# One broadcast of 784 KB in place of eight of 98 KB, and two buffer rings resized, in a graph-network layer on one core

## The chip, the cores and the metric

The kernel runs on one core of one Trainium2 chip. The time is device microseconds of one execution; the lower is the better. An execution counts from the program's launch to its end, and the profile's span, from the first instruction to the last, is a little shorter.

## The reference, cut to what matters

```python
def _L0_gnn_ref(X, edge_index, edge_types, W_data, b_data, W_control, b_control, W_self, b_self):
    src, dst = (edge_index[0], edge_index[1])
    Xs = X[src]
    m_data = Xs @ W_data.T + b_data
    m_ctrl = Xs @ W_control.T + b_control
    msg = jnp.where((edge_types == 0)[:, None], m_data, m_ctrl)
    agg = jax.ops.segment_sum(msg, dst, num_segments=X.shape[0])
    out = agg + (X @ W_self.T + b_self)
    return jax.nn.relu(out)
...
x = _layernorm(x + _L0_gnn_ref(...), axis=-1)
```

X has 6250 nodes of 128 float32 values. There are 100000 edges, sorted by `dst`, with a random `src` and a random type of two. Each node sums the messages of its edges; a message is the source's row times one of two weight matrices.

## The kernel before, in words

**The message table.** For every node both possible messages are computed once, each split into three bfloat16 parts (`m3`, 128 x 98 x 384, kept in SBUF). A copy goes to DRAM as `table`, whose rows the gathers read.

**Two ways to sum.** Nodes 0 to 4319 are cut into 27 ranges of 160 nodes (`WN`), and these lie in eight groups of 1, 2 and six times 4 ranges (`GROUPS`). The other 1930 nodes are cut into 16 blocks of 125.

*A range* is summed with matrix products alone. `ranks` sorts a group's edges by their source tile: it builds one-hot matrices (`hots`, L691), counts with TensorE (L702), reads the slot of each edge from the counts on VectorE (L716), and scatters the edges' source and target numbers into a small matrix of 32 slots x 98 columns per range. That matrix, 6272 bytes for each range, is written to DRAM as `packed` (L772). `sums` then loads it back, broadcast to all 128 partitions, as the tile `rows` (128 x 3136 bfloat16, 784 KB; the ring has three buffers). VectorE turns `rows` into a one-hot matrix in place (L912, two halves). TensorE selects messages with it (L933, "stage 1"), the result is copied from PSUM (L436 on ScalarE or L437 on VectorE), and a second product with the one-hot matrix of the targets (`hot2`, L920; products L947 and L950) adds them up. Messages that did not fit a slot come in `gl`, copied from a gather (L861, L868).

*A block* is summed from gathered rows. GpSimd's indirect DMA fetches 128 rows of `table` at a time into a buffer `t_msg` (L1027, 263 gathers, 98 KB each). VectorE makes the one-hot matrices of up to six gathers at once in a buffer `t_hot` (L1021, 47 of them). TensorE multiplies the two (L1034).

**What sets the order.** Nothing is issued as it is written. Every step is handed to a planner (`Plan`, L92) with an engine, an estimated duration, a due time, the buffers that it reads and writes, and `lat`, an estimate of the time to its data. `Plan.run` (L136) lets each engine take, of the steps that it believes to be ready, the one that is due first; the order that results is fixed in the program. Each engine then works through its order strictly, and a step whose data are not there holds up all that stands behind it on that engine. For a load of `rows` the planner believes in 0.45 us of the SyncE queue (`SPD`, L274) for each transfer, and in 2.0 us (`lat`, L908) plus 0.12 us (`HOP`, L93) from there until another engine may use it. These constants are the same whatever the size of a transfer is.

```python
RP, RA, RS = 8, 14, 0.9
...
for j in range(RP):
    add("SP", SPD, lambda i=i, sp=sp, j=j: S.dma_start(
        sp.t[P // RP * j : P // RP * (j + 1)].rearrange("p r c -> p (r c)"),
        packed[gi, i // 2, (i % 2) * 64 : (i % 2) * 64 + R, :]
        .rearrange("r c -> (r c)")[None, :].to_broadcast([P // RP, R * NT])),
        due - RA + RS * j, [(packed_b, gi)], [(sp, ("p", j))], lat=2.0)
```

L912 of a range reads all of `rows`, so it waits for the last of its eight transfers.

Of the kernel before, what the change touches and what calls it, by code (L numbers as in the profile page):

```python
# [11 lines left out]
BF16 = mybir.dt.bfloat16  # L12
# [9 lines left out]
P = 128  # L22
D = 128
D3 = 3 * D
# [67 lines left out]
class Plan:  # L92
# [10 lines left out]
    def add(self, engine, dur, fn, due, r=(), w=(), lat=0.0):  # L103
        alts = engine if isinstance(engine, list) else [(engine, dur, fn)]
        op = Op(alts, due, lat)
        op.index = len(self.ops)
        kind = [(i[0] if isinstance(i, tuple) else i).name for i in w] or ["out"]
        if engine == "SP" and due > self.FROM:
            op.slack = self.SLACK.get(kind[0], 0.0)
        self.ops.append(op)  # L110
        deps = set()
        for items, writes in ((r, False), (w, True)):
            for item in items:
                b, key = item if isinstance(item, tuple) else (item, None)
                for k, (ws, rs) in b.keys.items():
                    if key is None or k is None or k == key:
                        deps.update(ws)
                        if writes:
                            deps.update(rs)
                if writes and key is None:  # L120
                    b.keys = {}
                ws, rs = b.keys.setdefault(key, ([], []))
                if writes:
                    b.keys[key] = ([op], [])
                else:
                    rs.append(op)
                if not b.users or b.users[-1] is not op:
                    b.users.append(op)
        deps.discard(op)
        op.deps = list(deps)  # L130
        return op
# [116 lines left out]
def sums_over_windows(ctx, tc, x, xt, edges, w, bias, out, total):  # L248
# [4 lines left out]
    work = ctx.enter_context(tc.tile_pool(name="work", bufs=2))  # L253
# [8 lines left out]
    def B(pool, shape, dtype, name, bufs=1, room=None):  # L262
        return Buf(plan, pool, shape, dtype, name, bufs, room)
# [8 lines left out]
    G0, G1 = 0.0, -4  # L272
    GC = 1.3
    SPD = 0.45  # L274
    RP, RA, RS = 8, 14, 0.9


    r0 = C([125, RH, 1], I32, "r0")
# [18 lines left out]
    def vec(due, cols, fn, r, w, rate=1.04):  # L297
        return add("DVE", dve(cols, rate), fn, due, r, w)
# [111 lines left out]
    def load_edges(b, n, out_, due, buf, key, engine):  # L410
        def fn():
            eng, typ = {"SP": (S, SP), "ACT": (A, ACT), "POOL": (G, mybir.EngineType.Pool)}[engine]
            if b:
                at = nc.values_load(
                    first.t[0:1, b : b + 1], engines=(typ,), min_val=0, max_val=E - n,
                    skip_runtime_bounds_check_because="it counts edges and is held to E - n")
                src = edges[ds(at, n), :]
            else:
                src = edges[:n, :]
            eng.dma_start(out_(), src.rearrange("(p k) c -> p k c", k=n // P))  # L420
        dur = (2.0 if engine == "POOL" else 1.6) if b else SPD
        add(engine, dur, fn, due, [first] if b else [], [(buf, key)], lat=2.0)
# [91 lines left out]
    def own(o, lhs, n):  # L514

        qs = [(j, min(R, n - R * j)) for j in range(-(-n // R))]
        for j, m in qs:
            T.matmul(o(j, m), lhs(j, m), w_sb.t[:, 2 * D :], start=False, stop=False,
                     skip_group_check=True)
        for j, m in qs:  # L520
            T.matmul(o(j, m), one3.t[:, :m], brows.t[:, 2 * D :], start=False, stop=False,
                     skip_group_check=True)
# [446 lines left out]
    def gathered(bis, when, step):  # L969

        nt, k_ = GT[bis[0]], len(bis)
        n = nt * k_
        gi = len(GROUPS) + bis[0]
        top = GB * max(GT)
        raw = B(work, [P, k_, nt, 3], I32, "t_raw", 2, 3 * top)
        for j, bi in enumerate(bis):
            load_edges(NW + bi, nt * P, lambda j=j: raw.t[:, j], when - 14 + 0.1 * j, raw, j,
                       "POOL" if bi < GB else "SP")
        G2 = lambda name, dt=F32: B(work, [P, k_, nt], dt, "t_" + name, 1, top)
        rel, lows, ins, far = (G2(k) for k in ("rel", "lows", "ins", "far"))  # L980
        cb, idx = G2("cb", I32), B(work, [P, n], I32, "t_idx", 2, top)
        code = B(work, [P, n, 2], BF16, "t_code", 2, 2 * top)
        d = when - 8
        nn = min(GN, N - NW * WN - GN * bis[0])
        fl = lambda b: b.t.rearrange("p b k -> p (b k)")
        f2 = lambda b: fl(b)[:, :, None].to_broadcast([P, n, 2])
        vec(d, n, lambda: V.tensor_sub(
            rel.t, raw.t[:, :, :, 1], gbase.t[:, bis[0] : bis[0] + k_, None].to_broadcast(
                [P, k_, nt])), [raw, gbase], [rel])
        vec(d, n, lambda: V.tensor_single_scalar(lows.t, rel.t, nn + 0.5, op=ALU.is_lt), [rel],  # L990
            [lows])
        vec(d, n, lambda: V.scalar_tensor_tensor(
            ins.t, rel.t, 0.5, lows.t, op0=ALU.is_ge, op1=ALU.mult,
            accum_out=counts.t[:, gi : gi + 1]), [rel, lows], [ins, (counts, gi)])
        vec(d, n, lambda: V.tensor_single_scalar(cb.t, raw.t[:, :, :, 0], 7,
                                                 op=ALU.arith_shift_right), [raw], [cb])
        vec(d, n, lambda: V.tensor_single_scalar(far.t, raw.t[:, :, :, 2], 0.0,
                                                 op=ALU.not_equal), [raw], [far])
        vec(d, n, lambda: V.tensor_add(far.t, far.t, cb.t), [far, cb], [far])
        vec(d, n, lambda: V.scalar_tensor_tensor(  # L1000
            idx.t.rearrange("p (b k) -> p b k", k=nt), far.t, 128.0, raw.t[:, :, :, 0],
            op0=ALU.mult, op1=ALU.add), [far, raw], [idx])
        vec(d, 2 * n, lambda: V.tensor_tensor(code.t, f2(rel), f2(ins), op=ALU.mult), [rel, ins],
            [code])
        KB = 6
        got = []
        for j, bi in enumerate(bis):
            n0 = NW * WN + bi * GN
            xc = B(work, [D, P], F32, "t_xc", 2)
            start = when + step * nt * j  # L1010
            add("SP", SPD, lambda xc=xc, n0=n0: S.dma_start(xc.t[:, :nn], xt[:, n0 : n0 + nn]),
                start, m3_key(NS - 1), [xc], lat=2.5)
            ga = B(ps, [P, 512], F32, "ga", 1)
            for k in range(nt):
                at = start + step * k
                kk = j * nt + k
                if k % KB == 0:
                    kn = min(KB, nt - k)
                    hot = B(work, [P, kn, P], BF16, "t_hot", 3, KB * P)
                    s4 = [P, kn, P // 2, 2]  # L1020
                    vec(at + 1, kn * P, lambda hot=hot, kk=kk, kn=kn, s4=s4: V.tensor_tensor(  # L1021
                        hot.t.rearrange("p k (c d) -> p k c d", d=2),
                        iota1_b.t[:, :P].rearrange("p (c d) -> p c d", d=2)[:, None]
                        .to_broadcast(s4), code.t[:, kk : kk + kn, None, :].to_broadcast(s4),
                        op=ALU.is_equal), [code, (iota1_b, 0)], [hot], 0.52)
                m = B(work, [P, D3], BF16, "t_msg", 11)
                add("POOL", GC, lambda m=m, kk=kk: G.indirect_dma_start(  # L1027
                    out=m.t, out_offset=None, in_=table[:, :],
                    in_offset=bass.IndirectOffsetOnAxis(ap=idx.t[:, kk : kk + 1], axis=0)),
                    at, [idx, table_b], [m], lat=3.0)  # L1030

                def mm(m=m, hot=hot, k=k, ga=ga):
                    for i in range(-(-nn // R)):
                        T.matmul(ga.t[R * i : R * i + R, :D3], hot.t[:, k % KB, R * i : R * i + R],  # L1034
                                 m.t, start=k == 0, stop=False, skip_group_check=True)
                add("PE", 0.165, mm, at + 4.5, [hot, m], [ga])
            end = start + step * nt + 6
            add("PE", 0.3, lambda ga=ga, xc=xc: own(
                lambda i, m: ga.t[R * i : R * i + m, :D],
                lambda i, m: xc.t[:, R * i : R * i + m], nn), end, [xc, w_sb, one3, brows], [ga])  # L1040
            got.append((ga, end))
        close("g", NW * WN + bis[0] * GN, nn, nn, got, [], end + 2)
# [184 lines left out]
```

## Time and profile before

| | |
|---|---|
| time, median of three runs (534.1 to 541.71) | 538.46 us |
| the profiled execution: its time / its span | 538.46 us / 536.9 us |
| TensorE products (PE), busy | 460.6 us, 86% of the span |
| VectorE (DVE), busy | 395.0 us, 74% |
| ScalarE (ACT), busy | 354.8 us, 66% |
| GpSimd (POOL), busy | 299.6 us, 56% |
| mean granted TensorE clock | 0.962 |
| loads of `rows` on the SyncE queue (L904) | 216 transfers of 98 KB |

The page gives, by engine, line and operation, the busy time, the mean duration, and the idle time before the instructions with what ended it. "A <- B" in the list of waits says that A stood idle until B had ended; three numbers follow: the sum in us, how often, and the longest. SPq is the SyncE queue, which issues nearly all plain transfers. A transfer's issue and its landing are separate: the queue goes on once the transfer is issued.

### The profile page before, as it was taken

To read this page: it belongs to the slowest core of one execution; us is meant where nothing else is said; L and a number is where in the kernel's file an instruction comes from. 1 tells how busy PE (TensorE), PEld (TensorE's weight loads), DVE (VectorE), ACT (ScalarE), POOL (GpSimd) and SP (SyncE) were. 2 spreads that over 40 slices of the span, in tenths; PEclk is the share of its full clock that TensorE was granted. 3 is DMA by queue.
4 is the path that set the end of the run, shared out by engine and by line. 5 is a ranking of instruction groups with operands and counts; after the bars stand their busy time and mean duration, and the time that the engine had idled before them with its cause. 6 is when DMAs were issued, how large, how long until landed. Compare 5 with 4: busy or idle time off the path is not lost.

```text
span 536.9 us, 27273 instructions
## 1 busy us (share of the span) xinstructions
PE 460.6 (86%) x11461; PEld 370.6 (69%) x11461; DVE 395.0 (74%) x1273; ACT 354.8 (66%) x889; POOL 299.6 (56%) x290
## 2 busy tenths in 40 slices
PE   5999966997789989898798999679979799769991
PEld 3665644865668878687587878468868677558980
DVE  6898976997879879797488996657948569363333
ACT  3565844674557868677376787456877558668991
POOL 1100077767575757567575667455776727776700
PEclk9999989998989999999799999798999989999997
DMA  4699797359782796629946288471597715975410
GB/s 132 188 245 349 236 154 188 99 137 172 145 160 58 146 195 141 178 54 158 189 113 166 56 166 174 107 172 45 122 174 150 169 31 119 184 151 143 96 45 19
DMA packets 66144, 76.87 MB, mean 143 GB/s; under 512 B 24024, under 2 KB 55917, under 8 KB 66013
## 3 DMA queue, kind: packets, MB, share of 16 engines
q1 hardware_dynamic: 52171, 47.36, 39.0%
q0 software_dynamic: 13456, 27.42, 23.3%
q8 instruction: 92, 1.51, 1.3%
q14 instruction: 39, 0.32, 0.2%
q10 hardware_dynamic: 386, 0.26, 0.2%
HBM read 60.50 MB, written 13.17 MB: 137 GB/s over the span
## 4 chain that ended last, share of the span: by engine, by line
PE 57%; DMA 20%; ACT 6%; DVE 6%; SPq 6%; issue 3%; POOL 1%; ACTq 0%; DVEq 0%
PE g L933 16%; PE a L947 15%; DMA rows<-packed 11%; PE rk L702 6%; PE ga L1034 6%; SPq L904 4%; ACT gs L436 3%; PE a L950 3%; PE vt L752 2%; ACT to_d L443 2%; DVE rows L912 2%; DMA gl<-sr 2%; DMA xr<-in_x 2%; PE g L493 2%; DMA t_msg<-table,t_idx 1%
## 5 line engine op out<-in xcount | busy, mean ns | idle before, releaser
L1027 POOL DMA_INDIRECT t_msg<-table,t_idx x263 | 280.3, 1066 | 186.1 <-PE ga L1034 76.1
L436 ACT CAST gs<-g 128x384 bf16<-128x384 f32 x640 | 275.0, 482 | 110.7 <-PE g L933 91.8
L947 PE MATMUL a<-gs,hot 128*32 128x384 bf16 x2592 | 258.6, 336 | 12.5 <-DVE gs L437 4.6
L933 PE MATMUL g<-m,rows 128*32 128x384 bf16 x2646 | 260.3, 336 | 3.1 <-DVE rows L912 1.3
L933 PEld LDWEIGHTS <-rows 128*32 128x32 bf16 x2646 | 166.4, 135 | 21.0 <-issue 6.8
L950 PE MATMUL a<-gs,hot 128*32 128x128 bf16 x1944 | 163.8, 222 | 1.7 <-issue 1.7
L947 PEld LDWEIGHTS <-hot 128*32 128x32 bf16 x2700 | 119.7, 97 | 37.7 <-issue 21.3
L1034 PE MATMUL ga<-t_msg,t_hot 128*32 128x384 bf16 x1036 | 104.8, 334 | 2.3 <-DMA t_msg<-table,t_idx 1.9
L950 PEld LDWEIGHTS <-hot 128*32 128x32 bf16 x2025 | 84.7, 98 | 8.2 <-issue 2.2
L702 PE MATMUL rk<-hots,rest 128*32 128x392 bf16 (+1 forms) x556 | 57.6, 331 | 33.5 <-DVE slot L716 32.6
L912 DVE TENSOR_SCALAR rows<-rows,pid 128x1568 bf16<-128x1568 bf16 x54 | 34.8, 657 | 68.1 <-DMA rows<-packed 38.0
L716 DVE TENSOR_REDUCE slot<-rk 128x4 f32<-128x392 f32 (+1 forms) x138 | 76.3, 553 | 11.1 <-PE rk L702 9.1
L920 DVE TENSOR_TENSOR hot<-iota_b,to_d 128x1280 bf16<-128x1280 bf16 (+1 forms) x81 | 67.4, 840 | 0.1
L702 PE MATMUL rk<-hots,tri 128*32 128x392 bf16 (+1 forms) x588 | 62.6, 328 | 1.4 <-issue 1.4
L702 PEld LDWEIGHTS <-rest 128*32 128x32 bf16 x624 | 25.7, 97 | 44.9 <-issue 42.5
L1034 PEld LDWEIGHTS <-t_hot 128*32 128x32 bf16 x1036 | 49.6, 99 | 8.5 <-issue 4.1
L691 DVE TENSOR_TENSOR hots<-iota_b,st 128x784 bf16<-128x784 bf16 (+1 forms) x83 | 39.1, 486 | 0.7 <-PE vt L752 0.6
L561 DVE TENSOR_REDUCE s<-a 128x128 f32<-128x384 f32 x27 | 15.0, 555 | 27.5 <-ACT bs L436 23.6
L1021 DVE TENSOR_TENSOR t_hot<-iota_b,t_code 128x768 bf16<-128x768 bf16 (+2 forms) x47 | 24.6, 523 | 10.6 <-PE ga L1034 8.9
L702 PEld LDWEIGHTS <-tri 128*32 128x32 bf16 x672 | 28.6, 99 | 4.3 <-issue 1.8
L752 PEld LDWEIGHTS <-two 128*64 128x64 bf16 x567 | 14.7, 111 | 7.4 <-DVE two L743 2.4
L861 POOL DMA_INDIRECT sr<-table,at x14 | 15.3, 1092 | 6.7 <-DVE at L849 3.0
(188 smaller groups left out, 528.0 us busy)
## 6 DMA issues: line engine op xcount, KB each, us to landing
rows<-packed SPq DMA_DIRECT2D x216, 98.0 KB
table<-m SPq DMA_DIRECT2D x12, 768.0 KB
t_msg<-table,t_idx POOLq DMA_INDIRECT x263
rows<-in_xt SPq DMA_DIRECT2D x8, 256.0 KB
xc<-in_xt SPq DMA_DIRECT2D x6, 320.0 KB
gl<-sr SPq DMA_DIRECT2D x27, 48.0 KB
xr<-in_x SPq DMA_DIRECT2D x5, 256.0 KB
out<-xr SPq DMA_DIRECT2D x5, 256.0 KB
```

What stands on the lines that cost most here:

```text
L436: [("ACT", act(cols), lambda: A.copy(o(), src())), ("DVE", dve(cols), lambda: V.tensor_copy(o(), src()))], None, None, due, r, w, lat)
L691: lambda k=k, kn=kn, ci=ci, hs4=hs4: V.tensor_tensor(hv(ci)[:, k - ks[ci] : k - ks[ci] + kn].rearrange("p k w (c d) -> p (k w) c d", d=2), ...
L702: T.matmul(acc.t[R * j : R * j + R, c * wide : c * wide + wide], wt.t[:, R * j : R * j + R], one(k).rearrange("p w c -> p (w c)"), start=s ...
L716: vec(due, len(m) * wide, lambda r=r, m=m: V.tensor_reduce(slot.t[:, r:KT:L, :], acc.t[:, : len(m) * wide].rearrange("p (k w c) -> p k w c ...
L752: T.matmul(vv()[q : q + 64, i // 2, :], two.t[:, (k - k0) * nw + i].rearrange("p f r -> p (f r)"), one(k)[:, i, :], start=k == 0 and i < 2 ...
L912: add("DVE", dve(half * NT, 0.335), lambda sp=sp, rs=rs: V.tensor_scalar(sp.t[:, rs], sp.t[:, rs], pid1.t, None, op0=ALU.is_equal), due - ...
L920: lambda i=i, hot2=hot2, s4=s4, c0=c0, c1=c1: V.tensor_tensor(hot2.t[:, c0:c1].rearrange("p g (c d) -> p g c d", d=2), iota1_b.t.rearrange ...
L933: T.matmul(gp.t[R * t : R * t + R, :D3], sp.t[:, :, 4 * g + t], m3.t[:, 4 * g + t, :], start=True, stop=True)
L947: T.matmul(a.t[R * j : R * j + R, :D3], hot2.t[:, g, R * j : R * j + R], gs.t, start=g == 0, stop=False, skip_group_check=True)
L950: T.matmul(a.t[R * c : R * c + R, D3:], hot2.t[:, g, P:], gs.t[:, c * D : (c + 1) * D], start=False, stop=last, skip_group_check=True)
L1027: add("POOL", GC, lambda m=m, kk=kk: G.indirect_dma_start(out=m.t, out_offset=None, in_=table[:, :], in_offset=bass.IndirectOffsetOnAxis(a ...
L1034: T.matmul(ga.t[R * i : R * i + R, :D3], hot.t[:, k % KB, R * i : R * i + R], m.t, start=k == 0, stop=False, skip_group_check=True)
```

## The change

Three constants differ. A range's `rows` is loaded by one transfer to 128 partitions instead of eight transfers to 16 partitions each (`RP` 8 to 1). The ring of `t_hot` has two buffers instead of three, and the ring of `t_msg` has fourteen instead of eleven. The planner runs again with these, so the order of all engines' instructions is made anew. With `RP` at 1 the due time of the one load is that of the first of the eight before (14 us ahead of the range's own due time).

```diff
-    RP, RA, RS = 8, 14, 0.9
+    RP, RA, RS = 1, 14, 0.9
...
-                    hot = B(work, [P, kn, P], BF16, "t_hot", 3, KB * P)
+                    hot = B(work, [P, kn, P], BF16, "t_hot", 2, KB * P)
...
-                m = B(work, [P, D3], BF16, "t_msg", 11)
+                m = B(work, [P, D3], BF16, "t_msg", 14)
```

## The prediction

> **What bounds the kernel now.** I read the page's busy times first, then the groups by line, the list of waits, the timeline of one load of `rows`, and the busy times of three stretches.
>
> ```profile
> PE 460.6 (86%) x11461; PEld 370.6 (69%) x11461; DVE 395.0 (74%) x1273; ACT 354.8 (66%) x889; POOL 299.6 (56%) x290
> ```
>
> TensorE is the busiest, and 536.9 - 460.6 = 76.3 us of the span are left in which it does nothing. No change of this kind makes its work shorter, so whatever is to be won lies in these 76.3 us. VectorE has 0.31 us of work an instruction (395.0 / 1273).
>
> ```profile
> L912 DVE TENSOR_SCALAR rows<-rows,pid 128x1568 bf16<-128x1568 bf16 x54 | 34.8, 657 | 68.1 <-DMA rows<-packed 38.0
> L716 DVE TENSOR_REDUCE slot<-rk 128x4 f32<-128x392 f32 (+1 forms) x138 | 76.3, 553 | 11.1 <-PE rk L702 9.1
> L1021 DVE TENSOR_TENSOR t_hot<-iota_b,t_code 128x768 bf16<-128x768 bf16 (+2 forms) x47 | 24.6, 523 | 10.6 <-PE ga L1034 8.9
> ```
>
> Behind the bar stand the busy time and the mean duration, behind the second bar the idle time ahead of the group: VectorE stood idle for 68.1 us ahead of the 54 halves of L912, twice the time that they work. The list of waits says what ended it, and who on TensorE then waited for VectorE:
>
> ```profile
> DVE rows L912 <- DMA rows<-packed: 38.0, 14, 4.8
> PE rk L702 <- DVE slot L716: 32.6, 16, 4.5
> DVE rows L912 <- DMA gl<-sr: 12.1, 4, 4.1
> DVE rows L912 <- DMA xc<-in_xt: 4.8, 1, 4.8
> PE a L947 <- DVE gs L437: 4.6, 2, 4.2
> DVE rows L912 <- DMA xr<-in_x: 4.3, 2, 4.1
> DVE rows L912 <- DMA t_xc<-in_xt: 4.0, 1, 4.0
> DVE rows L912 <- DMA t_raw<-in_edges: 3.1, 1, 3.1
> PE g L933 <- DVE rows L912: 1.3, 1, 1.3
> ```
>
> L912 reads nothing that arrives by `gl`, `xc`, `xr`, `t_xc` or `t_raw`; those transfers use the same semaphores, so I read all six rows as waits for `rows`: 38.0 + 12.1 + 4.8 + 4.3 + 4.0 + 3.1 = 66.3 us. The three rows of TensorE behind VectorE sum to 38.5 us, half of its 76.3. They are mostly not waits for `rows` itself: L702 needs the slot of L716, which stands behind L912 in VectorE's order. One case, from the timelines of SyncE, VectorE and TensorE:
>
> ```profile
> 65.09 10.42 SPq L904 DMA_DIRECT2D rows<-packed  x16
> 71.11 0.56 DVE L716 TENSOR_REDUCE slot<-rk 128x4 f32<-128x392 f32 x1
> 75.19 0.63 DVE L912 TENSOR_SCALAR rows<-rows,pid 128x1568 bf16<-128x1568 bf16 x1 [3.52 <-DMA rows<-packed]
> 76.21 0.56 DVE L716 TENSOR_REDUCE slot<-rk 128x4 f32<-128x392 f32 x1
> 76.82 0.52 PE L702 MATMUL rk<-hots,rest 128*32 128x392 bf16 x4 [3.65 <-DVE slot L716]
> ```
>
> SyncE begins a range's eight issues at 65.09. VectorE comes to L912 at 75.19 - 3.52 = 71.67, which is 6.6 us later, and stands still for 3.52 us. TensorE then stands still for 3.65. So 66.3 us of VectorE's stalls cost TensorE 38.5, a share of 0.58.
>
> **The part that matters: one transfer for eight.** It removes 189 of 216 issues. At 10.42 / 16 = 0.65 us each while they follow one another, the eighth is issued 4.6 us after the first; with one transfer that wait is gone. What does the data itself take? The stretches tell (columns: length, busy times of five engines, clock, share of the DMA engines' time, GB/s):
>
> ```profile
> 67.00:72.00 5.00, 4.82 (x135) 3.97 (x131) 4.67 (x10) 3.85 (x10) 2.98 (x2) 1.00 1.02 147
> 385.00:398.00 13.00, 11.31 (x327) 9.78 (x326) 8.01 (x23) 10.16 (x26) 10.26 (x10) 1.00 1.02 183
> 40.00:54.00 14.00, 13.28 (x150) 8.33 (x148) 12.60 (x30) 8.05 (x15) 0.00 (x0) 1.00 1.05 341
> ```
>
> The DMA engines' time is used up in all three (1.02 to 1.05), but they move 147 GB/s while the eight transfers of `rows` run and 341 when transfers to or from all 128 partitions run. In the packet records the 16 packets of a lone 16-partition transfer take about 0.3 us each, and 0.77 us when several follow. Two readings fit: the writes into so few partitions at a time are slow (then one transfer to 128 partitions runs at up to 341 GB/s), or the common source of 6272 bytes is (then it stays at 147).
>
> The fixed part comes from the chain:
>
> ```profile
> 216.89 3.93 DMA rows<-packed
> 287.81 3.21 DMA rows<-packed
> ```
>
> An eighth transfer with little ahead of it took 3.21 us from its issue to L912 (98 KB, 0.10 MB). One of 0.80 MB (784 KB) takes 3.21 + 0.70 / 341 = 5.3 us at best and 3.21 + 0.70 / 147 = 8.0 us at worst. I take 5.6, near the best, because a lone 16-partition transfer starts fast and slows down when more follow, which a slow source would not do. Before, from the first issue to L912 it was 10.1 us here (75.19 - 65.09).
>
> But the planner does not know this. By its constants the data are there 8 x 0.45 + 2.12 = 5.7 us after the first issue, and now 0.45 + 2.12 = 2.6 us after the only one. It puts L912 there if VectorE has nothing due sooner. In the built order the first range of groups two to eight has its L912 now 5, 14, 21, 9, 10, 7 and 8 VectorE instructions earlier, 10.6 on average, or 3.3 us. For these seven ranges VectorE came 6.6 to 8.7 us after the first issue, 7.7 on average; now 4.4. Against 5.6 us a stall of 1.2 us stays, 7 x 1.2 = 8.4. The second range of a group is now issued right behind the first, 0.45 us later, instead of after seven more issues; it lands about 0.70 / 341 = 2.1 us after the first, and its L912 stands some ten instructions (3.1 us) behind the first's, so nothing stays. Third and fourth ranges wait for a free buffer of `rows` as before, and their L912 is not moved ahead; 0. The very first range keeps its 1.3. Sum: 9.7 us of 66.3 stay, 56.6 go, and TensorE gains 56.6 x 0.58 = 32.8 us.
>
> What becomes of them? TensorE held up less comes sooner to its other waits. No row prices that; the bounds are nothing and all of it, and I take three tenths back, nearer to nothing since VectorE and ScalarE have a quarter and a third of their time free. That leaves 23 us.
>
> The removed issues on SyncE also let the transfers queued behind them (`gl`, `xb`, `win`, `out`) go some 4 us sooner. TensorE's one wait for `gl` is 3.1 us; I count nothing. One cost on the other side: 0.80 MB now stand as one block ahead of the table and x loads at 29 us and of gathers elsewhere. Gathers have room: in the trace they are issued 5 to 24 us ahead of their first product, and TensorE waited for one for 1.9 us in all. I count nothing; without that cover it would be 2 to 5 us at up to 27 places.
>
> [...]
>
> [...]
>
> **The two rings.** With fourteen `t_msg` buffers GpSimd runs further ahead. It waits 76.1 us for L1034 now, but is busy only 56% and TensorE waits 1.9 us for it: 0. With two `t_hot` buffers, 45 of the 47 fills must come after the products of the group but one before, not but two. In the trace each fill stands right behind the products that free its buffer, and 9 us or more ahead of its own; one group is 442 / 47 = 9.4 us, so the data still come in time. VectorE's wait there is 10.6 us now (the row of L1021); I take it unchanged.
>
> **Sum.** 538.46 (the profiled execution, which is also the median; 1.6 outside its span) - 23 = 515 us.
>
> **Rivals.** *The source is the limit.* The transfer takes 8.0 us. The seven stalls are 8.0 - 4.4 = 3.6 each, 25 us; second ranges land 4.8 us after the first and stall about 2 each, 14 us; with 1.3 about 41 stay, 25 go, x 0.58 x 0.7 = 10: 528 us. For it: 147 GB/s holds in a stretch with almost no other traffic. Against: the fast first packets.
>
> *The waits are only passed on.* TensorE is then held by ScalarE, its own order or the clock: 538 us. For it: ScalarE's copies (L436) take 482 ns where the code's plan has 375. Against: ScalarE is idle a third of the time.
>
> *The smaller `t_hot` ring costs more than is won.* VectorE's six waits at L1021 average 10.6 / 6 = 1.8 us. If all 45 later fills wait so, VectorE loses 81 us, TensorE 47, and 515 + 47 = 562 us. From 22 waits on (23 / 0.58 / 1.8) the kernel is slower than before. For it: each fill now follows products that are one group younger. Against: the planner places the fills anew, and only four rows of before were real stalls.
>
> **How the numbers follow.** The forecast has 0.60, the slow source 0.18, waits passed on 0.12, the smaller ring 0.10. The range goes from all 66.3 us won with nothing back (538 - 38 = 500) to 537, which takes in the slow source and part of the third case. Two per cent is 11 us (about what a measurement tells): below 527.7 lie nine tenths of the forecast and half of the slow source, 0.64; slower than 549 is the ring's case, 0.10; the rest, 0.26, is the same.
>
> **What would show it.** Right: idle time ahead of L912 near 10 us, all of it at the first range of a group; "PE rk <- DVE slot" below 12; some 300 GB/s while `rows` lands. Wrong: that rate near 147; L912 still above 40; or L1021's idle time above 40.

## The result and the profile after

The changed kernel takes 481.02 us (median of four executions, 478.18 to 483.65); the kernel before takes 540.09 us beside it (534.1 to 542.47). The ratio is 0.8938, with a 95% interval of 0.883 to 0.9047: faster. The forecast was 515 us with a range of 500 to 537; it had the side right and the size far too small. (Ratios set aside the executions of a kernel that lie over 1.5% above its fastest, here some of the kernel before, so they stand a little nearer to one than the medians' quotient.)

The profiled execution took 478.18 us, with a span of 476.5. From the page of the changed kernel, the busy times and the granted clock in 40 slices:

```profile
PE 442.0 (93%) x11461; PEld 362.7 (76%) x11461; DVE 393.0 (82%) x1271; ACT 354.1 (74%) x891; POOL 298.4 (63%) x290
PEclk9999999999999999999999999999999999999996
```

For the same clock line of the kernel before, look at the eights and sevens in it:

```profile
PEclk9999989998989999999799999798999989999997
```

The span is 536.9 - 476.5 = 60.4 us shorter, in two parts. TensorE stands still for 476.5 - 442.0 = 34.5 us where it was 76.3: 41.8 us. And it works for 442.0 us where it was 460.6, with the same 11461 products: 18.6 us. The forecast had reasons for the first part and had excluded the second ("no change of this kind makes its work shorter").

The groups by line and the list of waits of the changed kernel answer to the rows shown of before:

```profile
L912 DVE TENSOR_SCALAR rows<-rows,pid 128x1568 bf16<-128x1568 bf16 x54 | 34.2, 638 | 8.9 <-DMA rows<-packed 8.8
L1021 DVE TENSOR_TENSOR t_hot<-iota_b,t_code 128x768 bf16<-128x768 bf16 (+2 forms) x47 | 24.6, 523 | 11.8 <-PE ga L1034 11.6
```

```profile
DVE rows L912 <- DMA rows<-packed: 8.8, 6, 2.7
...
PE rk L702 <- DVE slot L716: 3.2, 6, 1.6
...
PE g L933 <- DVE rows L912: 1.3, 1, 1.3
...
PE a L947 <- DVE gs L437: 0.6, 1, 0.6
```

VectorE's idle time ahead of L912 is 8.9 us (before 68.1). TensorE's three waits for VectorE are 3.2 + 1.3 + 0.6 = 5.1 us (before 38.5). The row of L1021 is where it was (10.6 before).

Where did the 18.6 us of TensorE's work go? The clock records of the kernel before hold eight stretches at a granted clock of 0.50 ahead of its end, at 76.0, 127.2, 157.9, 260.3, 338.8, 362.7, 431.0 and 482.2 us. Six are 3.4 us long and two 6.8, together 34.1 us. The profiled execution of the changed kernel has none of these, only the one at its end that both have. The one at 338.8, in the busy times of two stretches of the kernel before (columns: length, busy times of five engines with their instructions, clock, share of the DMA engines' time, GB/s), and what stands right ahead of it on TensorE's timeline:

```profile
338.80:345.60 6.80, 4.83 (x78) 3.21 (x81) 6.19 (x16) 2.87 (x7) 2.59 (x3) 0.50 0.37 112
346.00:352.80 6.80, 6.73 (x182) 5.62 (x175) 4.50 (x10) 5.69 (x15) 3.14 (x4) 1.00 0.42 109
```

```profile
335.50 0.36 PE L933 MATMUL g<-m,rows 128*32 128x384 bf16 x4
...
335.88 0.36 PE L933 MATMUL g<-m,rows 128*32 128x384 bf16 x3
340.77 0.52 PE L702 MATMUL rk<-hots,rest 128*32 128x392 bf16 x4 [4.52 <-DVE slot L716]
341.05 0.56 PE L933 MATMUL g<-m,rows 128*32 128x384 bf16 x4
```

TensorE stood still for 4.52 us because VectorE was late; the clock fell during that wait; four products of L933 then took 0.56 us, where four had taken 0.36 before it. Over the whole execution the products of L933 and L947 last 526 ns where they lie wholly inside those stretches and 329 elsewhere, 1.6 times and not twice as long. TensorE is busy for 29.8 of the 34.1 us; an estimate of what the half clock cost is 29.8 x (1 - 329 / 526) = 11 us.

That leaves some 7 of the 18.6 us. Most of it lies in how busy time is counted: at full clock a product adds 0.31 us to it in the mean behind a gap and 0.04 us in a stream, and the kernel before has 63 gaps where the changed one has 46, which is 17 x 0.27 = 4.6 us. The rest is not assigned. So a stall of TensorE was paid more than once here: while it stood, and, where the clock fell, again while it worked on slowly.

When does the clock fall? In the clock records of before all eight stretches begin on one grid of 3.41 us. In the piece of that grid just ahead of each, TensorE was idle for 2.1 to 3.1 us, and in no other piece at full clock, from 11 us on to the last products, was it idle for more than 1.92. (In the four kernels of the square below the border lies in the same place, between 1.85 and 1.95 us, with one exception, a stretch behind a piece with 1.44.) So the length of one stall doesn't settle it: a stall of 1.32 us at 125.3 us, with smaller gaps beside it, was followed by a stretch, and one of 3.07 us at 84.7 us, which lies half in one piece and half in the next, was not. These are the pieces (idle is the length less the first busy time):

```profile
123.80:127.21 3.41, 1.31 (x24) 0.68 (x24) 2.69 (x11) 0.20 (x1) 2.80 (x3) 1.00 1.05 170
82.84:86.25 3.41, 1.49 (x37) 1.05 (x37) 2.59 (x8) 0.78 (x2) 2.51 (x3) 1.00 0.83 195
86.25:89.67 3.42, 1.87 (x49) 1.57 (x52) 1.14 (x3) 1.14 (x4) 2.51 (x4) 1.00 0.59 158
```

### The profile page after: what moved, and what is told of

Same layout as the page of the kernel before. It is cut to its first block, busy times and chain, and to the rows that moved or that the text cites. A ratio compares the mean times of both kernels' runs of the same rounds, so it can differ in the third digit from the quotient of the medians.

```text
span 476.5 us, 26926 instructions
## 1 busy us (share of the span) xinstructions
PE 442.0 (93%) x11461; PEld 362.7 (76%) x11461; DVE 393.0 (82%) x1271; ACT 354.1 (74%) x891; POOL 298.4 (63%) x290
## 4 chain that ended last, share of the span: by engine, by line
PE 73%; DVE 10%; ACT 7%; DMA 6%; issue 2%; SPq 0%; ACTq 0%; DVEq 0%
PE g L933 20%; PE a L947 19%; PE rk L702 9%; PE ga L1034 7%; ACT gs L436 4%; PE a L950 3%; PE vt L752 3%; DMA t_msg<-table,t_idx 3%; PE g L493 3%; DMA rows<-packed 2%; DVE hot L920 2%; PE a L493 2%; ACT to_d L443 2%; DVE slot L716 2%; PE ga L702 1%
## 5 line engine op out<-in xcount | busy, mean ns | idle before, releaser
L947 PE MATMUL a<-gs,hot 128*32 128x384 bf16 x2592 | 249.0, 328 | 7.7 <-ACT gs L436 5.1
L933 PE MATMUL g<-m,rows 128*32 128x384 bf16 x2646 | 253.0, 327 | 1.8 <-DVE rows L912 1.3
L933 PEld LDWEIGHTS <-rows 128*32 128x32 bf16 x2646 | 168.7, 134 | 13.1 <-DVE rows L912 1.6
L950 PE MATMUL a<-gs,hot 128*32 128x128 bf16 x1944 | 159.6, 219 | 0.2 <-issue 0.2
L947 PEld LDWEIGHTS <-hot 128*32 128x32 bf16 x2700 | 115.9, 95 | 33.9 <-issue 15.5
L1034 PE MATMUL ga<-t_msg,t_hot 128*32 128x384 bf16 x1036 | 102.0, 326 | 1.3 <-DMA t_msg<-table,t_idx 1.3
L716 DVE TENSOR_REDUCE slot<-rk 128x4 f32<-128x392 f32 (+1 forms) x138 | 76.3, 553 | 12.5 <-PE rk L702 9.8
L950 PEld LDWEIGHTS <-hot 128*32 128x32 bf16 x2025 | 82.5, 97 | 3.5 <-issue 0.4
L702 PE MATMUL rk<-hots,tri 128*32 128x392 bf16 (+1 forms) x588 | 59.9, 317 | 0.0
L702 PE MATMUL rk<-hots,rest 128*32 128x392 bf16 (+1 forms) x556 | 54.4, 320 | 4.9 <-DVE slot L716 3.2
L1034 PEld LDWEIGHTS <-t_hot 128*32 128x32 bf16 x1036 | 49.9, 97 | 5.5 <-issue 2.2
L912 DVE TENSOR_SCALAR rows<-rows,pid 128x1568 bf16<-128x1568 bf16 x54 | 34.2, 638 | 8.9 <-DMA rows<-packed 8.8
L1021 DVE TENSOR_TENSOR t_hot<-iota_b,t_code 128x768 bf16<-128x768 bf16 (+2 forms) x47 | 24.6, 523 | 11.8 <-PE ga L1034 11.6
L752 PE MATMUL vt<-hots,two 128*64 128x98 bf16 x546 | 17.1, 208 | 0.8 <-DVE two L743 0.4
```

The source lines that it names most:

```text
L702: T.matmul(acc.t[R * j : R * j + R, c * wide : c * wide + wide], wt.t[:, R * j : R * j + R], one(k).rearrange("p w c -> p (w c)"), start=s ...
L716: vec(due, len(m) * wide, lambda r=r, m=m: V.tensor_reduce(slot.t[:, r:KT:L, :], acc.t[:, : len(m) * wide].rearrange("p (k w c) -> p k w c ...
L752: T.matmul(vv()[q : q + 64, i // 2, :], two.t[:, (k - k0) * nw + i].rearrange("p f r -> p (f r)"), one(k)[:, i, :], start=k == 0 and i < 2 ...
L912: add("DVE", dve(half * NT, 0.335), lambda sp=sp, rs=rs: V.tensor_scalar(sp.t[:, rs], sp.t[:, rs], pid1.t, None, op0=ALU.is_equal), due - ...
L933: T.matmul(gp.t[R * t : R * t + R, :D3], sp.t[:, :, 4 * g + t], m3.t[:, 4 * g + t, :], start=True, stop=True)
L947: T.matmul(a.t[R * j : R * j + R, :D3], hot2.t[:, g, R * j : R * j + R], gs.t, start=g == 0, stop=False, skip_group_check=True)
```

## Experiments

The theory after the result: the one transfer does all of it, by taking away VectorE's stalls at L912 and with them the half-clock stretches. Rivals: the new order does it; the two rings do it; and, inside the first theory, it may be that there are fewer issues or that the writes go to all partitions at once.

The times differ from chip to chip. On one, the kernel before took 538.92 us, as in its first profile; on four others it took 678 to 689. So each kernel is compared with the kernel before on its own chip only. Each of these five chips was used at one time only, so the chip and the time are not told apart.

**A square: transfer and order, each alone.** First the changed kernel again.

> The changed kernel once more, beside the kernel before on this chip, as the mark for the three others here. If TensorE runs without the short gaps of its own that the last four runs showed (some 90 us of them), 481 us against 538 within 8 each. If it has them here too, the kernel before is near 690 us and this one at 0.98 to 1.0 of it, since the stalls at L912 then hide behind TensorE.

Then the one transfer in the order of before, with before's rings. The planner still believes in eight transfers; seven issue nothing:

```diff
-  add("SP", SPD, lambda i=i, sp=sp, j=j: S.dma_start(
-      sp.t[P // RP * j : P // RP * (j + 1)].rearrange("p r c -> p (r c)"),
+  add("SP", SPD, lambda i=i, sp=sp, j=j: j == 0 and S.dma_start(
+      sp.t.rearrange("p r c -> p (r c)"),
...
-      .rearrange("r c -> (r c)")[None, :].to_broadcast([P // RP, R * NT])),
+      .rearrange("r c -> (r c)")[None, :].to_broadcast([P, R * NT])),
```

> The order of before to the instruction, the first of a range's eight loads carrying all 784 KB. Theory A (the transfer makes the gain, in whatever order): within 10 us of the changed kernel on this chip, idle time ahead of L912 below 10 us. Theory C (the new order and the rings make it): nearer to the kernel before than to the changed one, above 510 us where that is 481 and 538.

And the reverse: order and rings of the changed kernel, but its one step issues the eight old transfers:

```diff
-  add("SP", SPD, lambda i=i, sp=sp, j=j: S.dma_start(
+  add("SP", SPD, lambda i=i, sp=sp: [S.dma_start(
-      sp.t[P // RP * j : P // RP * (j + 1)].rearrange("p r c -> p (r c)"),
+      sp.t[16 * k : 16 * (k + 1)].rearrange("p r c -> p (r c)"),
...
-      .rearrange("r c -> (r c)")[None, :].to_broadcast([P // RP, R * NT])),
+      [None, :].to_broadcast([16, R * NT])) for k in range(8)],
```

> The order of the changed kernel to the instruction, each load as eight transfers to 16 partitions. Theory A: not faster than the kernel before, 535 to 560 us where that takes 538; idle time ahead of L912 65 us or more, TensorE busy 458 us or more for the same products, clock at most 0.965. Theory C: 510 us or less.

**Eight transfers, but each to all partitions.** Order, rings and bytes of before. Each of the eight now writes an eighth of the columns (784 bytes) of all 128 partitions, where it wrote all 6272 bytes of 16 partitions:

```diff
-  sp.t[P // RP * j : P // RP * (j + 1)].rearrange("p r c -> p (r c)"),
...
-  .rearrange("r c -> (r c)")[None, :].to_broadcast([P // RP, R * NT])),
+  sp.t.rearrange("p r c -> p (r c)")[:, 392 * j : 392 * (j + 1)],
...
+  [None, 392 * j : 392 * (j + 1)].to_broadcast([P, 392])),
```

> The order of before to the instruction and eight transfers of 98 KB a range as there, but each goes to all 128 partitions (784 bytes of each) instead of all 6272 bytes of 16 partitions. Theory D (slow writes into few partitions at a time make the 147 GB/s): the rate while rows lands rises above 220 GB/s, idle time ahead of L912 falls to 10 to 25 us and the time to 485 to 505. Theory S (eight issues, whatever they carry): the idle time stays above 50 us and the time above 525.

What was measured, all on the same chip (before: median 538.92, 530.15 to 542.03, 13 executions; its profile is the first one):

| kernel | median us | ratio [95%] | idle ahead of L912, us | PE busy, us | PE idle, us | mean clock |
|---|---|---|---|---|---|---|
| before | 538.92 | | 68.1 | 460.6 | 76.3 | 0.962 |
| changed, again | 480.83 | 0.9011 [0.8924, 0.9098] | 7.2 | 443.6 | 37.3 | 0.988 |
| one transfer, order of before | 485.98 | 0.914 [0.9005, 0.9275] | 0.0 | 444.8 | 36.8 | 0.984 |
| eight transfers, order of after | 533.57 | 0.9967 [0.9896, 1.0038] | 70.9 | 461.0 | 73.8 | 0.962 |
| eight over all partitions, order of before | 504.42 | 0.9486 [0.9338, 0.9634] | 31.7 | 452.3 | 50.4 | 0.98 |

The one transfer is worth 538.92 - 485.98 = 52.9 us in the old order and 533.57 - 480.83 = 52.7 in the new. Order and rings together are worth some 5 us in either pair, and by the intervals that can't be told from nothing: with eight transfers the interval holds 1, with one transfer the two intervals overlap. The rivals "order" and "rings" fall as the cause of the large gain (the two were changed together here, so they are not told apart on this chip). What theory A expected held in both, but for 533.57 us where 535 or more were expected. The group of L912 in the profiles of one transfer in the old order, and of eight in the new:

```profile
L912 DVE TENSOR_SCALAR rows<-rows,pid 128x1568 bf16<-128x1568 bf16 x54 | 34.5, 652 | 0.0
```

```profile
L912 DVE TENSOR_SCALAR rows<-rows,pid 128x1568 bf16<-128x1568 bf16 x54 | 35.0, 654 | 70.9 <-DMA rows<-packed 47.5 <-DMA win<-in_edges 7.1 <-DMA out<-xr 6.4
```

In the old order no stall is left at all, which fits an L912 that has not been moved ahead; in the new order, 7 to 9 us are, as forecast, and the kernel is none the slower for it. The stretches at half clock (without the one at the end) follow: one in the changed kernel again, one with one transfer in the old order, eight (30.7 us) with eight transfers in the new order, three in the fourth kernel. So the second payment goes with the stalls, not with the order. With one transfer, the one stretch left in each of the two stands behind a wait of TensorE for a gather, of 2.7 and 3.1 us.

The fourth kernel was to part the two ways in which one transfer could help. Its order and its number of transfers are those of before, and 538.92 - 504.42 = 34.5 us of the 52.9 are won, about two thirds (60% by the ratios): so much goes with the spread of the writes over all partitions. The other 18 us go when eight issues become one. The parting is not clean, since the pieces written also shrink from 6272 to 784 bytes. And neither theory held whole: the time lies where theory D had it, but 31.7 us of idle time are more than its 10 to 25, and the rate, shown below, is not above 220 GB/s but 164. What the eight issues still cost is seen on its SyncE timeline, two ranges' issues in a row:

```profile
65.24 9.27 SPq L904 DMA_DIRECT2D rows<-packed  x16
```

How fast the data move, in the busy times of the stretch in which the second group's first two ranges land: first the changed kernel, then one transfer in the old order, eight over all partitions, and eight old transfers in the new order.

```profile
68.00:72.80 4.80, 3.09 (x83) 2.40 (x79) 2.64 (x7) 2.24 (x6) 3.22 (x4) 1.00 1.01 339
```

```profile
67.20:72.50 5.30, 5.12 (x139) 4.12 (x131) 5.30 (x12) 3.88 (x10) 3.66 (x4) 1.00 0.95 324
```

```profile
67.00:73.00 6.00, 5.74 (x160) 4.50 (x151) 5.93 (x13) 4.25 (x11) 4.10 (x3) 1.00 0.53 164
```

```profile
68.00:75.00 7.00, 1.98 (x52) 1.43 (x44) 0.37 (x2) 2.16 (x5) 4.93 (x6) 0.93 1.01 157
```

The last two columns are the reading. 157 GB/s at a share of 1.01: the DMA engines are full and slow. 164 GB/s at 0.53: they are half empty, the queue hands out transfers too slowly for them (9.27 / 16 = 0.58 us for each 98 KB allows no more than 173 GB/s). The rate is much the same in both, but in the fourth kernel the data land closer behind their issues: of these two ranges, the last packet was done at 77.7 us, and at 80.9 us in the kernel before, with the issues begun at 65.2 and 65.1. 324 to 339 at 0.95 to 1.01: full and fast. In the packet records, a packet of 6272 bytes takes 520 ns in the median before and 240 ns after.

**On the other chips.** Here each part was tried alone. One transfer alone is the kernel before with only `RP` at 1 (order made anew); rings alone has only `t_hot` at 2 and `t_msg` at 14; "planner told" is the changed kernel with the estimate of a load raised:

```diff
-  due - RA + RS * j, [(packed_b, gi)], [(sp, ("p", j))], lat=2.0)
+  due - RA + RS * j, [(packed_b, gi)], [(sp, ("p", j))], lat=4.6)
```

First chip, with the two kernels of the square:

> Kernel before with the one transfer of 784 KB alone; the rings stay at 3 (t_hot) and 11 (t_msg). Theory A (the transfer is all of it): idle time ahead of L912 near 9 us, granted clock near 0.99, 481 us within 8. Theory B (the rings, or the order that they bring, give a good part): 492 us or more, with GpSimd waiting for L1034 near 76 us as before.

> Kernel before with the two rings alone (t_hot 2, t_msg 14), eight transfers as before. Theory A: idle time ahead of L912 stays at 60 to 70 us, 538 us within 8. Theory B: 528 us or less. If the smaller t_hot ring costs something, the idle time ahead of L1021 rises above 20 us and the time above 546.

> The order is that of the changed kernel, to the instruction; each of its 27 loads is issued as eight transfers to 16 partitions, one behind the other. Theory A: L912 stands 3.3 us sooner in VectorE's order at the first range of a group, so the idle time ahead of L912 is at least that of before, 65 to 90 us; 540 to 560 us, granted clock 0.96 or less, TensorE busy 458 us or more for the same products (it is 442 in the changed kernel). Theory C: 505 us or less.

> The order of all engines is that of before, to the instruction; of a range's eight loads the first now carries all 784 KB to 128 partitions and the other seven are not issued. Theory A (the transfer itself): VectorE comes to L912 7.7 us after the issue on average and the data need 5 to 6, so the idle time ahead of L912 falls below 10 us; 481 us within 8, clock near 0.99. Theory C (the new order makes the gain): 505 us or more.

Second chip:

> The changed kernel, as the mark for the three others here: 481 us within 4, idle time ahead of L912 7 to 9 us.

> The changed kernel with one constant more: the planner is told that the load of rows takes 4.6 us (lat) instead of 2.0, close to the 4.0 to 5.5 us from issue to the last packet of a load with nothing ahead of it. Theory P (the 7 to 9 us left ahead of L912 at first ranges of groups still cost): idle time ahead of L912 below 3 us, and 3 to 8 us less than the changed kernel, 473 to 478. Theory Q (TensorE is the bound now, so the rest is covered, or the new order takes it back): within 3 us of the changed kernel, or slower.

> The kernel before with the one transfer alone, planned as such; rings 3 and 11. If the two rings make the 5 us between the changed kernel (481) and the one transfer in the order of before (486), this one is near 486; if the order that the planner makes for one transfer does, it is near 481.

> The kernel before with the two rings alone, eight transfers. If the rings are worth 5 us, 534 against 539; if not, 539 within 4. A cost of the smaller t_hot ring would show as idle time ahead of L1021 above 20 us and a time above 545.

Third chip:

> The changed kernel as the mark: 481 us within 4 where the kernel before takes 539; near 1.02 of the kernel before where that takes some 680.

> The changed kernel with the planner told 4.6 us instead of 2.0 for the load of rows. Theory P (the left stall costs): idle time ahead of L912 below 3 us, 3 to 8 us less than the changed kernel. Theory Q (covered, or given back by the new order): within 3 us of it, or slower.

> One transfer alone, rings 3 and 11. Rings make the 5 us: near 486. The order for one transfer makes it: near 481.

> The two rings alone, eight transfers. Rings make the 5 us: near 534. Not the rings: 539 within 4.

Fourth chip:

> The changed kernel with the planner told 4.6 us instead of 2.0 for the load of rows, against the changed kernel's 0.901 of the kernel before. Theory P (the left stall costs): 0.885 to 0.895 of the kernel before, idle time ahead of L912 below 3 us. Theory Q (covered or given back): 0.897 or more. Where the kernel before takes some 680 us, 1.01 to 1.02 of it.

> The two rings alone, eight transfers. Rings make the 5 us: 0.99 of the kernel before. Not the rings: 1.00 within 0.006. Where the kernel before takes some 680 us, 1.02 of it as in the two calls so far.

| ratio to before [95%] | first (before 689.48) | second (678.03) | third (688.19) | fourth (686.22) |
|---|---|---|---|---|
| one transfer alone | 0.9904 [0.9873, 0.9936] | 0.9953 [0.9925, 0.9982] | 0.9887 [0.9848, 0.9926] | |
| one transfer, order of before | 0.9901 [0.9869, 0.9933] | | | |
| rings alone | 1.0161 [1.0119, 1.0204] | 1.0219 [1.0161, 1.0278] | 1.0176 [1.0152, 1.02] | 1.016 [1.0098, 1.0222] |
| eight transfers, order of after | 1.0139 [1.0088, 1.0189] | | | |
| changed kernel | | 1.0179 [1.0127, 1.023] | 1.0111 [1.0069, 1.0154] | |
| changed kernel, planner told | | 1.0238 [1.0181, 1.0295] | 1.0191 [1.0122, 1.026] | 1.017 [1.0118, 1.0222] |

None of these chips gave the times of the first result, so they don't answer its question, but they show that the gain hangs on more than the transfer. Where an expectation named such chips for a part (1.02 for the rings, 1.01 to 1.02 with the planner told), it held. The changed kernel is 1.1 to 1.8% slower than before there. One transfer is worth only 0.5 to 1.1%, and the rings cost 1.6 to 2.2%. Where the kernel spends its time there, in the same 60 us of the changed kernel, first on the chip of the square, then on the third of these:

```profile
200.00:260.00 60.00, 58.56 (x1646) 49.84 (x1639) 53.37 (x162) 47.38 (x120) 45.86 (x45) 1.00 0.55 162
```

```profile
200.00:260.00 60.00, 46.06 (x1044) 32.28 (x1037) 36.50 (x126) 32.59 (x83) 26.53 (x27) 0.91 0.33 101
```

TensorE gets through 1044 products instead of 1646. That VectorE, fed by it, therefore comes to L912 later fits what follows, but was not tried by itself. This is the group of L912 with eight old transfers (rings alone, first chip):

```profile
L912 DVE TENSOR_SCALAR rows<-rows,pid 128x1568 bf16<-128x1568 bf16 x54 | 33.4, 629 | 16.3 <-DMA rows<-packed 12.0 <-issue 2.5 <-DMA xc<-in_xt 1.8
```

16.3 us of stalls (29.3 with eight transfers in the order of after) where the other chip has 68 to 71, so there is little to win. Telling the planner gains nothing: its intervals overlap those of the changed kernel where both ran. Why TensorE is slower on these chips, and why the rings cost there, stays open. VectorE's idle time ahead of L1021 doesn't settle it: on the first chip it is 43.9 us with the rings alone, but 43.1 and 49.3 with three buffers and one transfer (order of before, and order made anew). The half-clock stretches (109.8 us in all with one transfer alone, 139.4 with the rings alone, on the first chip, with the stretch at the end) show the effect and not its cause.

## Why the prediction was wrong

**The step that failed** is the sentence "No change of this kind makes its work shorter, so whatever is to be won lies in these 76.3 us": TensorE's busy time fell by 18.6 us, some 11 of them by the clock. The second is the term "three tenths back", 9.8 us, of which 2.4 were found. The path through VectorE, which gave the forecast its side, was right.

**The stalls that stay: right.** 9.7 us were forecast ahead of L912, at the first ranges of the groups, and 8.9 and 7.2 were measured, with one wait of 1.4 us elsewhere (the third range of the last group) and none at the very first range, for which 1.3 had been forecast. The transfer was taken at 5.6 us from issue to L912; its packets were all done 4.0 to 5.5 us after the issue where nothing was ahead of it. The rate was to be "some 300 GB/s" and was 306 to 339. The rival "the source is the limit" (147 GB/s) fell with that.

**The share of 0.58: nearly right.** The clean test is one transfer in the order of before. It takes away all 68.1 us of VectorE's idle time, and TensorE's waits for VectorE in the three rows fall from 38.5 to 2.6 us: a share of 35.9 / 68.1 = 0.53. (TensorE's whole idle time falls by 76.3 - 36.8 = 39.5, which is 0.58 again, but by luck: other waits went and came in it.) In the changed kernel TensorE's waits for VectorE fell by 38.5 - 5.1 = 33.4 us, against 32.8 forecast.

**"Three tenths back": wrong.** Almost nothing came back. TensorE's waits for ScalarE went from 4.4 to 5.1 us, and one for VectorE at L574 (1.7) is new. That is 2.4 against 33.4. The other way, two small items went that the forecast had at nothing: the wait for `gl` (3.1 us before, which was named) and TensorE's own "issue" idle time (8.4 us before, 1.7 after), which was not named. So the idle part is 41.8 instead of 23. A likely reason stands in the forecast itself, that VectorE and ScalarE had a quarter and a third of their time free; no run tested it.

**The missing term: the clock.** The forecast priced a stall by its own length. The trace of before had the second price in it: 34.1 us at a granted clock of 0.50, an estimated 11 us of work lost over eight stretches (2% of the span of 536.9), each stretch begun within a stall of TensorE or at most 1.2 us behind one, and each of these stalls was a wait for VectorE. I had read the mean clock (0.962) and not asked where the missing part lay. With 33 + 11 the sum would have been 538 - 44 = 494; the wait for `gl`, the issue time and the other 7 us of busy time make up most of what is left to 481.

**Rings and order: nothing forecast, at most 5 us found** on the chip of the forecast, not told from nothing. "VectorE's wait there is 10.6 us now, I take it unchanged" held (11.8 and 14.0). The rival that ended slower, the smaller `t_hot` ring, asked for over 40 us ahead of L1021 and fell there. GpSimd's wait for L1034 fell from 76.1 to 18.2 us, but to 30.4 with eleven buffers and one transfer, so most of that is not the ring's.

**Gathers: right for the changed kernel.** TensorE waited for `t_msg` for 1.3 us, before 1.9. A delay of gathers behind the block of 0.80 MB, which the prediction put at 2 to 5 us without cover, is not seen: a gather's packets of 4608 bytes take 267 ns in the median, before 318, and from the end of a gather's instruction to its last packet it is 1.93 us in the median and 5.06 at most, before 2.08 and 5.85. The cover is not sure, though: the changed kernel again waited 2.7 us for gathers, and the one transfer in the order of before 5.5, though its gathers landed no later (1.78 in the median, 5.59 at most).

**The reading of slow writes to few partitions: the right direction.** Several transfers to 16 partitions each were slow (147 GB/s at a DMA share of 1.02 before, 157 at 1.01 in the order of after), and eight transfers over all partitions alone win 34.5 of 52.9 us, some two thirds. The first transfer of a range, in the kernel before, had its 98 KB done 1.03 us (median) after its first packet began, which is 97 GB/s. What makes the writes to few partitions slow was not measured.

## What to carry to other kernels

When TensorE stands still for some 2 us out of 3.4, as it did ahead of each of the eight stretches here (2.1 to 3.1 of 3.41), read the granted clock behind it, stretch by stretch, and add what the half-clock stretch loses to the price of the stall; a mean clock of 0.962 hid it here. Before a broadcast is cut into pieces, compare GB/s with the DMA share: here full and slow (157 GB/s at 1.01) went with the shape of the writes, half empty (164 at 0.53) with the issues. Cut along the columns, this load cost less (504.42 us) than cut along the partitions (538.92), and whole it cost least (485.98). And a gain of this kind seems to need a consumer that is fast enough to wait: on the chips where TensorE was slower (on the third, 1044 products in 60 us instead of 1646), the one transfer won 0.5 to 1.1%.

## What the runs showed of the hardware that was not expected

Transfers of 98 KB into 16 partitions each filled the DMA engines (a share of 1.01 to 1.02) at 147 to 157 GB/s; the same bytes to 128 partitions in one transfer ran at 306 to 339 (a share of 0.93 to 1.01), with 240 ns instead of 520 for a packet of 6272 bytes. The granted clock fell to 0.50 for the next 3.41 us or more after TensorE had idled for some 2 us of a 3.41 us piece (2.1 to 3.1 in the kernel before; one exception at 1.44 in the square), and products of L933 and L947 then took 1.6 times as long (526 ns against 329). And the time of this kernel differed by more than a quarter from chip to chip (each used at one time only): before took 538.92 us on one and 678 to 689 on four, at an equal length of a product at full clock (328 and 329 ns for L933 and L947 in the changed kernel) but with more time at half clock, 124.6 against 13.9 us with the stretch at the end, and 1044 against 1646 products in the same 60 us.
